# A graph attention layer on one core: exponentials in mid-step, joined rows loaded within the loop, quotients ahead in the last stage

## The chip, the core and the metric

The kernel runs on one core of one Trainium2 chip. The metric is the device time of one execution in microseconds, as the median of three runs. Five engines work beside each other, each on a queue of its own in program order: TensorE (PE, matrix products and transposes, with PEld for its weight loads), VectorE (DVE), ScalarE (ACT), GpSimd (POOL, here the issuer of indirect transfers) and SyncE (SP, the issuer of most other transfers). An instruction that waits holds up everything behind it on its engine.

## The reference

There are 12,500 nodes with 128 features and 400,000 edges, sorted by their target `dst`. For each edge:

```
h       = relu(layernorm(x))
message = (h @ w_src + b_src)[src] + (h @ w_dst)[dst]
message = message * edge_weight * radial_mlp(edge_attr_32)      # 32 -> 64 -> 64 -> 128, silu
message = message @ w_sep + b_sep                               # 8 heads x (16 alpha + 16 value)
score   = sum(smooth_leaky_relu(alpha) * alpha_dot)             # one per head
att     = segment_softmax(score, dst)                           # over the edges of one target
out     = segment_sum(value * att, dst) @ w_proj + b_proj
x       = x + out
```

The softmax's maximum and sum run over all edges with the same target, wherever they lie in the sorted list.

## The kernel before

**Tiling.** The edges are cut into 782 sections of 512; two sections are a pair, and the main loop takes one pair `k` per step, 391 (`NP`) steps. Features or channels lie on partitions, edges along the free dimension. Three constants order the loop: `MP = 8` pairs share one softmax group, `r = k % 8` is the step's place in its group, and `LAG = 13` is the number of steps by which the weighted values and their sums (`c = k - LAG`) run behind the messages of pair `k`.

**One step.** The order of the calls in `step(k)` is written by hand, and every engine follows it. `gather(k + 2)` (L867) has POOL bring 128 source rows per indirect transfer, eight per pair, into three buffers `gs0` and `gs1` for each half. `sources(k)` (L934) transposes the rows of this step on PE, which frees a buffer. `mlp1`, `mlp2` and `mlp3` (L886, L901, L918) are the radial net for pairs `k + 2`, `k + 1` and `k`, with `silu` on ACT (L890, L904; L904 comes once a step). `message` (L941, L948) adds the target rows and multiplies. `alphas` and `alphas_sum` (L954, L956, L961) make the activation of pair `k - 1`. In odd steps `scores` (L970, L987) makes the scores of two pairs; they go through a DRAM buffer `sc_d`, and at a group's end come back as `S` (L993) in another layout. `values` (L1065, L1067) multiplies the values of pair `c` with their weights, `one_hot` (L1051, L1054) marks the targets, and `sums` (L1078, L1082) adds them up into `ob` for a window of 64 nodes per section.

**The softmax group.** Once in eight steps, at the end of a step: `softmax_up` at `r = 2` (a product that spreads marks, L1003, and a running maximum on DVE, L1008), `softmax_down` at `r = 3` (L1013), then `softmax_exp` (subtraction on DVE, L1018, and the exponential on ACT, L1020). `softmax_T` at `r = 4` transposes the result (L1035) and copies it (L1038). ACT loads a table ahead of the exponential and another ahead of the next `silu`.

**Joining the windows.** Each section's sums are stored in section order into `agg`, the table of node rows (`store`, L1090), and whole windows into `win` (`store_win`, L1086). A target whose edges cross a section's end needs its parts joined. Thirteen blocks of 128 section ends do that (`block_load` to `block_out`, at fixed steps of the loop given by `LATE` and `stages`); eleven are finished in the loop and kept in `obs_d`. Behind the loop each is loaded into `comb` (L1364) and scattered by node number into `agg` (`scatter`, L1197), one per step of the 14 steps that bring the lagging values to an end; the last two blocks are made there. The tile framework orders accesses to `agg` by itself, unless a group declares that there is no dependence; in that queue a store waits for the scatter before it and the other way round.

**The last stage.** `final` loads `agg` in nine pieces of up to twelve blocks of 128 nodes (L1401), divides by the sum of weights (`quotients`: L1411, L1412, L1413 on DVE), and for 25 quads of four blocks transposes (L1424), copies (L1427), multiplies with `w_proj` (L1435), adds `x` (L1438) and stores (L1439). The quotients of the next twelve blocks are asked for in the middle of the three quads before.

Of the kernel before, what the change touches and what calls it, by code (L numbers as in the profile page):

```python
# [51 lines left out]
MQ = 2 * MP  # L52
LAG = 13


@with_exitstack
def gnn_kernel(ctx: ExitStack, tc: tile.TileContext, a: dict, out: bass.AP):
# [694 lines left out]
    def windows():  # L752
# [7 lines left out]
        with tc.tile_pool(name="ps", bufs=1, space=PSUM) as pp, \  # L760
# [254 lines left out]

            def softmax_exp(m):
                M = Ms[m]
                nc.vector.tensor_sub(M[:, 0, :], S_all[m], M[:, 1, :])  # L1018
                Ps[m] = sp.tile([P, SEC], F32, name="Pr", bufs=1)
                nc.scalar.activation(Ps[m], M[:, 0, :], AF.Exp)  # L1020
# [64 lines left out]
            def store_win(c):  # L1085
                nc.sync.dma_start(out=win[c * P:(c + 1) * P, :], in_=accs[c])  # L1086

            def store(c, f):
                at = nc.sync.value_load(base[0:1, f, c:c + 1])
                st = nc.sync.dma_start(out=agg[ds(at, W - 1), :], in_=accs[c][f * W:(f + 1) * W - 1, :])  # L1090
# [47 lines left out]
            def block_maxima(g):  # L1138
                w, node = width(g), nodes.pop(g)
                differ[g] = sp.tile([P, P + 1], BF16, name="differ", bufs=1)  # L1140
                nc.vector.tensor_tensor(differ[g][:, 0:w], node[:, 1:w + 1], node[:, 0:w], op=ALU.not_equal)
# [10 lines left out]
            def block_factors(g):  # L1152
# [4 lines left out]
                nc.vector.tensor_sub(mx, mx, up[:, 1:1 + w])  # L1157
                nc.scalar.activation(de, de, AF.Exp)
                nc.scalar.activation(mx, mx, AF.Exp)
                nc.vector.tensor_mul(mx[:, 1:w:2], mx[:, 1:w:2], differ.pop(g)[:, 1:w:2])  # L1160

            def block_columns(g):
# [6 lines left out]
                nc.tensor.transpose(pt[:, 1, 0:w], rx[:w, :], ident[:w, :w])  # L1169
                mx = mxs.pop(g)  # L1170
                tots[g] = [sp.tile([P, P], F32, name=n, bufs=2) for n in ("rn", "rd")]
                for k, r in enumerate(tots[g]):
# [22 lines left out]
            def scatter(g):  # L1195
# [5 lines left out]
                tc.declare_no_dep(st.ins, group="combined", reason="each node's row is written once")  # L1201
                tc.add_to_no_dep_group("combined", st.ins)

            comb = {}

            def combined(g):
# [3 lines left out]
            stages = {0: lambda g: (block_load(g), block_rows(g)), 2: block_maxima, 4: block_factors,  # L1210
                      5: block_columns, 6: block_totals, 8: block_out}
            assert LAST_M * MP == (NC - 1) * SB and NP - LAST_M * MP < MP and LATE + (NC - 3) * SB + 8 < NP

# [7 lines left out]
            def step(k):  # L1221
# [55 lines left out]
                if has(k + 2):  # L1277
                    mlp1(k + 2)
                if has(k):
                    mlp3(k)  # L1280
# [4 lines left out]
                if has(c - 1):  # L1285
                    sums(c - 1)
                    if k >= NP:
                        store_win(c - 1)
                        store(c - 1, 0)
                        store(c - 1, 1)  # L1290
# [37 lines left out]
                j, o = divmod(k - LATE, SB)  # L1328
                if 0 <= j < NC - 2 and o in stages:
                    stages[o](j)  # L1330

            for k in range(-5, NP):
                step(k)
            held.close()

# [6 lines left out]
            def out_rows(g):  # L1342
                block_rows_out(g, combined(g))
                scatter(g)

            jobs = {
                0: lambda: block_load(last - 1),
                1: lambda: block_maxima(last - 1),
                2: lambda: block_factors(last - 1),
                5: lambda: block_load(last),  # L1350
                6: lambda: block_maxima(last),
                7: lambda: (block_factors(last), block_rows(last - 1)),
                8: lambda: block_columns(last - 1),
                9: lambda: block_totals(last - 1),
                10: lambda: out_rows(last - 1),
            }
            assert SB * (NC - 1) + LAG + 1 == NP + 7
# [12 lines left out]
            block_rows(last)  # L1370
            block_columns(last)
# [7 lines left out]

    XQ = 12  # L1380
    out_v = out[0:NF * P, :].rearrange("(p t) c -> p t c", t=NF)
# [10 lines left out]
    def final(fp, x_fin, turned, product):  # L1392
        starts = list(range(0, NB, XQ))
        gs, qs, qTs = {}, {}, {}

        def load_g(i):

            gs[i] = fp.tile([P, XQ, ROW], F32, name="g", bufs=len(starts))
            for n, t0, t1 in blocks(starts[i], min(starts[i] + XQ, NB)):
                o = starts[i]  # L1400
                nc.sync.dma_start(out=gs[i][:n, t0 - o:t1 - o, :],  # L1401
                                  in_=agg_v[:, t0:t1, :] if n == P else agg[NF * P:N, :].unsqueeze(1))

        def quotients(i):
            r = fp.tile([P, XQ, H], F32, name="r")
            qs[i] = fp.tile([P, XQ, C], F32, name="q")
            g = gs.pop(i)
            for n, t0, t1 in blocks(starts[i], min(starts[i] + XQ, NB)):
                s = slice(t0 - starts[i], t1 - starts[i])
                m = t1 - t0  # L1410
                nc.vector.tensor_scalar(r[:n, s, :], g[:n, s, C:ROW], 1e-16, None, op0=ALU.add)  # L1411
                nc.vector.reciprocal(r[:n, s, :], r[:n, s, :])  # L1412
                nc.vector.tensor_mul(  # L1413
                    qs[i][:n, s, :].rearrange("p t (h k) -> p (t h) k", h=H),
                    g[:n, s, 0:C].rearrange("p t (h k) -> p t h k", h=H),
                    r[:n, s, :].unsqueeze(3).to_broadcast([n, m, H, C // H]))

        def turn(i):
            t0, t1 = quads[i]
            q, o = qs[t0 // XQ], t0 // XQ * XQ  # L1420
            pt = turned(i)
            for t in range(t0, t1):
                n = rows(t)
                nc.tensor.transpose(pt[:, t - t0, :n], q[:n, t - o, :], ident[:n, :n])  # L1424
            w = (t1 - t0 - 1) * P + rows(t1 - 1)
# [97 lines left out]
```

## Time and profile before

| | |
|---|---|
| three runs | 4210.71, 4211.2, 4215.71 us; median 4211.2 |
| the profiled execution's own time | 4210.06 us |
| its span, from the first to the last instruction | 4208.2 us |
| PE, DVE, POOL, ACT busy | 3917.1 (93%), 3103.4 (74%), 3009.4 (72%), 1901.6 (45%) us |
| mean granted clock of PE | 0.978 |
| first and last gather start | 73.65 and 4009.50 us |
| last stage, first quotient to last sum | 4142.28 to 4201.67 us |

The profile is of one execution. A row of a timeline gives the start in the span, the duration, engine, line, operation, what is written from what, and in brackets how long the engine was idle before and what ended that. A row of a group gives busy time and mean duration in ns, then the idle time before its instructions with what ended it. PE's busy time is that of pipelined products with modelled ends. Idle time on an engine that nobody waits for costs nothing.

### The profile page before, as it was taken

Reading aid. Unit: us, or ns where it says so; the run is one execution under the profiler, and the core shown is the slowest. Engines: PE = TensorE matmul, PEld = TensorE weight load, DVE = VectorE, ACT = ScalarE, POOL = GpSimd, SP = SyncE. Lnnn points to the kernel's source line nnn. Section 1 sums busy time; section 2 is a strip of 40 time slices with the busy share of each in tenths; the row PEclk is TensorE's granted clock in tenths of the full one; section 3 lists DMA queues with packets and bytes.
Section 4 is the critical chain, followed back from the end, with each engine's and each line's share of the span. In section 5 each row is a group of like instructions: output and inputs, shape, how many; then the busy total and the mean of one; then the engine's idle time right before and its main releaser. Section 6 shows DMA issues by size and latency. Waiting matters only on the chain. (4 is left out here: it accounts for less than half of the span.)

```text
span 4208.2 us, 87881 instructions
## 1 busy us (share of the span) xinstructions
PE 3917.1 (93%) x29351; PEld 2391.0 (57%) x29351; DVE 3103.4 (74%) x6187; ACT 1901.6 (45%) x4549; POOL 3009.4 (72%) x3195
## 2 busy tenths in 40 slices
PE   6789999999999999999999999999999999999975
PEld 6345555555555555555555555555555555555555
DVE  5567777777777777777777777777777777777754
ACT  5344444444444444444444444444444444444421
POOL 4767777777777777777777777777777777777710
PEclk8999999999999999999999999999999999999988
DMA  7766777777776776777777776776777676776624
GB/s 249 233 173 187 191 187 187 197 192 180 199 192 179 196 195 174 195 195 188 188 192 194 181 193 180 178 188 182 178 191 184 183 184 183 188 180 180 184 84 160
DMA packets 593334, 783.08 MB, mean 186 GB/s; under 512 B 125554, under 2 KB 392303, under 8 KB 592741
## 3 DMA queue, kind: packets, MB, share of 16 engines
q1 hardware_dynamic: 384786, 514.16, 40.9%
q0 software_dynamic: 100416, 205.44, 23.6%
q10 hardware_dynamic: 107666, 57.76, 4.6%
q8 instruction: 234, 3.83, 0.4%
q14 instruction: 232, 1.89, 0.2%
HBM read 637.83 MB, written 139.30 MB: 185 GB/s over the span
## 5 line engine op out<-in xcount | busy, mean ns | idle before, releaser
L867 POOL DMA_INDIRECT gs<-t_src,idx x3125 | 2971.5, 951 | 978.8 <-issue 801.7
L956 ACT ACTIVATE sl<-pa,c_b_a 128x512 f32<-128x512 f32 x782 | 536.9, 687 | 1021.1 <-PE pa L954 1009.5
L961 DVE SCALAR_TENSOR_TENSOR al<-pa,sl 128x512 f32<-128x512 f32 x782 | 539.8, 690 | 596.6 <-ACT sl L956 577.1
L1065 PEld LDWEIGHTS V<-c_w_v,mT 128*128 128x128 f32 x6048 | 746.7, 194 | 292.1 <-DVE ob L1082 119.1
L1065 PE MATMUL V<-c_w_v,mT 128*128 128x128 f32 x6048 | 879.3, 289 | 0.0
L954 PE MATMUL pa<-mT,c_w_a 128*128 128x512 f32 x1564 | 816.1, 604 | 4.0 <-DVE mT L948 3.0
L1067 DVE TENSOR_TENSOR pvx<-V,Pem 128x512 f32<-128x512 f32 x756 | 517.7, 685 | 243.8 <-PE V L1065 232.0
L934 PEld LDWEIGHTS pm<-ident,gs 128*128 128x128 f32 x3125 | 393.0, 142 | 422.1 <-issue 316.9
L1078 PEld LDWEIGHTS misc<-pvx,oh 128*64 128x64 f32 x6250 | 353.0, 137 | 407.8 <-ACT h L890 392.7
L926 DVE SCALAR_TENSOR_TENSOR rad<-p,c_fc_b,w_b 128x512 f32<-128x512 f32 x782 | 550.0, 745 | 40.1 <-PE p L918 3.5
L1078 PE MATMUL misc<-pvx,oh 128*64 128x136 f32 x6250 | 454.2, 287 | 115.4 <-ACT h L890 108.2
L948 DVE SCALAR_TENSOR_TENSOR mT<-pm,c_b_src,rad 128x512 f32<-128x512 f32 x782 | 550.6, 746 | 2.2 <-PE pm L941 2.2
L904 ACT ACTIVATE h<-p,b 128x512 f32<-128x512 f32 x391 | 287.6, 735 | 422.7 <-PE p L901 367.9
L934 PE MATMUL pm<-ident,gs 128*128 128x128 f32 x3125 | 471.0, 273 | 0.0
L918 PE MATMUL p<-h,w3b 64*128 64x512 f32 x1564 | 405.2, 595 | 14.4 <-ACT h L904 14.4
L941 PE MATMUL pm<-ohT,m 64*128 64x512 bf16 x2346 | 321.8, 380 | 0.0
L987 ACT ACTIVATE Sp<-m,b_s 128x512 f32<-128x512 f32 x192 | 131.9, 687 | 393.9 <-PE m L970 389.8
L886 PE MATMUL m<-eT,w1b 64*128 64x256 f32 x782 | 274.3, 431 | 17.9 <-DVE M L1008 16.7
L886 PE MATMUL misc<-eT,w1b 64*128 64x256 f32 x782 | 274.3, 431 | 0.0
L1051 DVE TENSOR_TENSOR oh<-lane,misc 128x504 f32<-128x504 f32 x391 | 261.3, 668 | 0.0
L901 PE MATMUL p<-h,w2b 64*64 64x256 f32 x3128 | 259.7, 402 | 1.0 <-DVE rad L926 1.0
L954 PEld LDWEIGHTS pa<-mT,c_w_a 128*128 128x128 f32 x1564 | 242.2, 196 | 20.0 <-DVE mT L948 7.1
(172 smaller groups left out, 3651.0 us busy)
## 6 DMA issues: line engine op xcount, KB each, us to landing
w_b<-in_edge_weight SPq DMA_DIRECT2D x390, 512.0 KB
d_b<-in_dst SPq DMA_DIRECT2D x390, 256.0 KB
gs<-t_src,idx POOLq DMA_INDIRECT x3125
e_t<-in_edge_attr ACTq DMA_DIRECT2D x390, 128.0 KB
sc_d<-Sp SPq DMA_DIRECT2D x192, 256.0 KB
win<-ob SPq DMA_DIRECT2D x391, 68.0 KB
agg<-ob SPq DMA_DIRECT2D x782, 33.5 KB
md<-t_dst SPq DMA_DIRECT2D x782, 32.0 KB
```

The lines of the kernel that those rows point to most:

```text
L867: nc.gpsimd.indirect_dma_start(out=gs[:, t, :], out_offset=None, in_=t_src[:, :], in_offset=bass.IndirectOffsetOnAxis(ap=idx[:, t0 + t:t0 ...
L886: nc.tensor.matmul(p1[q], w1b[s, :], eTs[k][s, :], start=True, stop=True)
L918: nc.tensor.matmul(p3s[k][:, f, 0:SEC], w3b[s, :], h2s[k][s, :], start=True, stop=True)
L926: nc.vector.scalar_tensor_tensor(rad[:, s], p3[:, f, 0:n], b3, w_g[k][:, s], op0=ALU.add, op1=ALU.mult)
L934: nc.tensor.matmul(pms[k, f][:, t * T:(t + 1) * T], gs[:, t, :], ident, start=(t == 0), stop=False, is_transpose=True, skip_group_check=True)
L948: nc.vector.scalar_tensor_tensor(mTs[k][:, s], pms.pop((k, f))[:, 0:n], b_n, rad[:, s], op0=ALU.add, op1=ALU.mult)
L954: nc.tensor.matmul(pa[:, 0:n], w_a, mTs[k][:, f * SEC:f * SEC + n], start=True, stop=True)
L956: nc.scalar.activation(sl[:, 0:n], pa[:, 0:n], AF.Silu, bias=b_a, scale=1.0)
L961: nc.vector.scalar_tensor_tensor(al, pa, 0.25, sl, op0=ALU.mult, op1=ALU.add)
L1065: nc.tensor.matmul(V[:, t, :], mTs[c][:, o:o + T], w_v, start=True, stop=True)
L1067: nc.vector.tensor_mul(pvx[c][:, f, 0:n, 0:C].rearrange("p t (h k) -> p t h k", h=H), V[:, 0:n, :].rearrange("p t (h k) -> p t h k", h=H), ...
L1078: nc.tensor.matmul(acc[f * W:(f + 1) * W, :], ohs[c][:, f * TS + t, :], pvx[c][:, f, t, :], start=(t == 0), stop=(t == n - 1), skip_group_ ...
```

## The change

Four things change together:

- `LAG` is 12. The softmax group is one step shorter: `softmax_up` moves to the middle of the step with `r = 2`, `softmax_down` and the subtraction (now `softmax_sub`) to its end, the exponential to the middle of the step with `r = 3` ahead of `mlp3`, and both `softmax_T` into that step. Table loads and exponentials of a block (`block_exp`) stand beside the large ones; the stages of a block are at other steps.
- The eleven finished blocks are loaded from `obs_d` in four transfers behind the steps `NP - 6` to `NP - 3`, into buffers of the edge loads (`bring`), and all are scattered behind the last gather. `order` declares by section which stores and scatters do not depend on each other.
- The rows of the last block are loaded two steps earlier as far as they exist; the last four come straight from `ob` (`last_rows_2`), not through `win`.
- In the last stage the pieces are of 1, 2 and then 3 quads, the quotients overwrite their inputs and are made up to four quads ahead of the sums, and transposes go two quads ahead.

```diff
-LAG = 13
+LAG = 12
+    EARLY_S = [(-(-2 * NS // P) - i) * (P // 2) for i in (2, 1)]
...
             def softmax_exp(m):
+                Ps[m] = sp.tile([P, SEC], F32, name="Pr", bufs=1)
+                nc.scalar.activation(Ps[m], Ms[m][:, 0, :], AF.Exp)
+
+            def softmax_sub(m):
                 M = Ms[m]
                 nc.vector.tensor_sub(M[:, 0, :], S_all[m], M[:, 1, :])
-                Ps[m] = sp.tile([P, SEC], F32, name="Pr", bufs=1)
-                nc.scalar.activation(Ps[m], M[:, 0, :], AF.Exp)
...
+            def order(ins, s, whole=False):
+                i = 1 if s < EARLY_S[0] else 2 if s < EARLY_S[1] else 3
+                for j in (1, 2):
+                    if j < i:
+                        tc.declare_no_dep(ins, group=f"early_{j}", reason="its rows follow those of the earlier sections")
+                    if i <= j:
+                        tc.declare_no_dep(ins, group=f"later_{j}", reason="its rows precede those of the later sections")
+                if whole and i < 3:
+                    tc.add_to_no_dep_group(f"early_{i}", ins)
+                if i > 1:
+                    tc.add_to_no_dep_group(f"later_{i - 1}", ins)
...
-                if 2 * c + 1 >= (NC - 1) * (P // 2):
-                    tc.declare_no_dep(st.ins, group="combined", reason="its rows follow those of the blocks")
+                order(st.ins, 2 * c)
...
+            def block_exp(g):
+                nc.scalar.activation(des[g], des[g], AF.Exp)
+                mx = mxs[g][:, 0:width(g)]
                 nc.scalar.activation(mx, mx, AF.Exp)
...
             stages = {0: lambda g: (block_load(g), block_rows(g)), 2: block_maxima, 4: block_factors,
-                      5: block_columns, 6: block_totals, 8: block_out}
+                      6: block_columns, 7: block_totals, 9: block_out}
...
+                if has(k - MP) and r == 3:
+                    softmax_exp(m - 1)
+                    if 0 <= j < NC - 2 and o == 5:
+                        block_exp(j)
                 if has(k):
                     mlp3(k)
...
+                if has(k - MP) and r == 2:
+                    softmax_up(m - 1)
                 if has(c):
                     values(c, 1)
-                if has(k - MP) and r == 4:
-                    softmax_T(m - 1, 0)
...
                     message(k)
+                if has(k - MP) and r == 3:
+                    softmax_T(m - 1, 0)
                 if has(k + 1):
                     mlp2(k + 1)
-                if has(k - MP) and r == 4:
-                    softmax_T(m - 1, 1)
                 if has(k - MP):
                     if r == 2:
-                        softmax_up(m - 1)
+                        softmax_down(m - 1)
+                        softmax_sub(m - 1)
                     elif r == 3:
-                        softmax_down(m - 1)
-                        softmax_exp(m - 1)
+                        softmax_T(m - 1, 1)
...
+            def bring(j):
+                g0, g1 = 3 * j, min(3 * j + 3, NC - 2)
+                t = lp.tile([P, 3, ROW], F32, name="e_t", bufs=4)
+                nc.sync.dma_start(out=t[:, 0:g1 - g0, :],
+                                  in_=obs_d[g0 * P:g1 * P, :].rearrange("(g p) c -> p g c", p=P))
+                for g in range(g0, g1):
+                    comb[g] = t[:, g - g0, :]
...
             for k in range(-5, NP):
                 step(k)
+                if 0 <= k - (NP - 6) < 4:
+                    bring(k - (NP - 6))
+                if k == NP - 3:
+                    for g in range(NC - 2):
+                        scatter(g)
...
+            def last_rows_2():
+                q = width(last) // 2
+                for i in range(2):
+                    nc.sync.dma_start(out=rrs[last][(i + 1) * q - 2:(i + 1) * q, :],
+                                      in_=accs[NP - 1][i * (W - 1):i * (W - 1) + W + 1:W, :])
...
-                if 0 <= j - 2 < NC - 2:
-                    nc.sync.dma_start(out=combined(j - 2), in_=obs_d[(j - 2) * P:(j - 1) * P, :])
-                    scatter(j - 2)
...
-        for i in range(len(starts)):
-            load_g(i)
-        quotients(0)
-        turn(0)
-        for i in range(Q):
-            if i % 3 == 1 and i // 3 + 1 < len(starts):
-                quotients(i // 3 + 1)
-            if i + 1 < Q:
-                turn(i + 1)
-            finish(i)
+        for j in range(len(parts)):
+            load_g(j)
+        made = 0
+        for i in range(-2, Q):
+            while made <= at[min(i + 4, Q - 1)]:
+                quotients(made)
+                made += 1
+            if i + 2 < Q:
+                turn(i + 2)
+            if i >= 0:
+                finish(i)
```

More of the change, by code (lines that the diff above doesn't have):

```diff
@@ L1139, in block_maxima @@
                 w, node = width(g), nodes.pop(g)
-                differ[g] = sp.tile([P, P + 1], BF16, name="differ", bufs=1)
+                differ[g] = sp.tile([P, P + 1], BF16, name="differ", bufs=2)
                 nc.vector.tensor_tensor(differ[g][:, 0:w], node[:, 1:w + 1], node[:, 0:w], op=ALU.not_equal)
@@ L1202, in scatter @@
                 tc.add_to_no_dep_group("combined", st.ins)
+                order(st.ins, g * (P // 2), True)
             comb = {}
@@ L1287, in step @@
                     if k >= NP:
-                        store_win(c - 1)
+                        if k == NP + LAG:
+                            last_rows_2()
+                        else:
+                            store_win(c - 1)
                         store(c - 1, 0)
@@ L1344, in out_rows, with last_rows @@
                 scatter(g)
+            def last_rows():
+                q, s = width(last) // 2, last * (P // 2)
+                rrs[last] = sp.tile([P, ROW], F32, name="rr", bufs=1)
+                for i in range(2):
+                    nc.sync.dma_start(out=rrs[last][i * q:(i + 1) * q - 2, :],
+                                      in_=rows_w[s:s + q - 2, i * (W - 1), :])
+            def last_rows_2():
+                q = width(last) // 2
+                for i in range(2):
+                    nc.sync.dma_start(out=rrs[last][(i + 1) * q - 2:(i + 1) * q, :],
+                                      in_=accs[NP - 1][i * (W - 1):i * (W - 1) + W + 1:W, :])
             jobs = {
@@ L1349, in windows @@
                 2: lambda: block_factors(last - 1),
[L1350 to L1355, printed above, removed]
+                3: lambda: block_exp(last - 1),
+                4: lambda: block_load(last),
+                5: lambda: block_maxima(last),
+                6: lambda: (block_factors(last), block_exp(last), block_rows(last - 1)),
+                7: lambda: block_columns(last - 1),
+                8: lambda: block_totals(last - 1),
+                9: lambda: out_rows(last - 1),
+                LAG - 1: last_rows,
             }
-            assert SB * (NC - 1) + LAG + 1 == NP + 7
+            assert SB * (NC - 1) + LAG + 1 == NP + 6
             for k in range(NP, NP + LAG + 1):
@@ L1369, in windows @@
                 pass
-            block_rows(last)
             block_columns(last)
@@ L1392, in final @@
     def final(fp, x_fin, turned, product):
[L1393 to L1411, printed above, removed]
+        ends_q = [1, 3] + list(range(6, Q, 3)) + [Q]
@@ new lines, in final, with load_g @@
+        parts = [(quads[a][0], quads[b - 1][1]) for a, b in zip([0] + ends_q, ends_q)]
+        at = [next(j for j, (t0, t1) in enumerate(parts) if t0 <= q0 < t1) for q0, _ in quads]
+        gs, qTs = {}, {}
+        def load_g(j):
+            t0, t1 = parts[j]
+            gs[j] = fp.tile([P, t1 - t0, ROW], F32, name=f"g{j}", bufs=1)
+            for n, u0, u1 in blocks(t0, t1):
+                nc.sync.dma_start(out=gs[j][:n, u0 - t0:u1 - t0, :],
+                                  in_=agg_v[:, u0:u1, :] if n == P else agg[NF * P:N, :].unsqueeze(1))
@@ L1412, in quotients @@
+        def quotients(j):
+            p0, p1 = parts[j]
+            r = fp.tile([P, 12, H], F32, name="r")
+            for n, t0, t1 in blocks(p0, p1):
+                s = slice(t0 - p0, t1 - p0)
+                nc.vector.tensor_scalar(r[:n, s, :], gs[j][:n, s, C:ROW], 1e-16, None, op0=ALU.add)
                 nc.vector.reciprocal(r[:n, s, :], r[:n, s, :])
[L1413 to L1416, printed above, removed]
+                q = gs[j][:n, s, 0:C].rearrange("p t (h k) -> p t h k", h=H)
+                nc.vector.tensor_mul(q, q, r[:n, s, :].unsqueeze(3).to_broadcast([n, t1 - t0, H, C // H]))
@@ L1418, in turn @@
         def turn(i):
             t0, t1 = quads[i]
-            q, o = qs[t0 // XQ], t0 // XQ * XQ
+            q, o = gs[at[i]], parts[at[i]][0]
             pt = turned(i)
@@ L1423, in turn @@
                 n = rows(t)
-                nc.tensor.transpose(pt[:, t - t0, :n], q[:n, t - o, :], ident[:n, :n])
+                nc.tensor.transpose(pt[:, t - t0, :n], q[:n, t - o, 0:C], ident[:n, :n])
             w = (t1 - t0 - 1) * P + rows(t1 - 1)
```

9 lines of the change are left out of this document (4 added, 5 removed).

## The prediction

> **What bounds the kernel now.** I read the page first, then the timeline of GpSimd (POOL) through the loop, then the steps of the loop on ScalarE (ACT) and TensorE (PE), then everything behind the last gather. The first row below is the page's group of gathers (busy, mean ns, idle before), the next four are POOL's timeline (start, us, what, idle before), the last is PE's.
>
> ```profile
> L867 POOL DMA_INDIRECT gs<-t_src,idx x3125 | 2971.5, 951 | 978.8 <-issue 801.7
> ...
> 73.65 1.18 POOL L867 DMA_INDIRECT gs<-t_src,idx  x1 [13.53 <-DMA t_dst<-ms]
> ...
> 4008.24 0.95 POOL L867 DMA_INDIRECT gs<-t_src,idx  x1 [0.30 <-issue]
> 4009.50 0.94 POOL L867 DMA_INDIRECT gs<-t_src,idx  x1 [0.30 <-PE V L1065]
> 4066.26 1.02 POOL L1197 DMA_INDIRECT agg<-comb,ids  x1 [55.82 <-PE pm L1065]
> 4035.72 0.27 PE L934 MATMUL pm<-ident,gs 128*128 128x128 f32 x1
> ```
>
> The gathers start 1.25 us apart (0.95 busy, 0.30 before it) and nothing but the next gather's own issue ends the time between them: eight steps of eight gathers cannot take less than 80.0 us. From the first to the last start 3124 intervals took 3935.9 us, 1.260 each. So most of the span runs at nearly the gathers' own pace; only 31 us (3935.9 - 3124 x 1.25) are lost to waits and slow gathers. The second thing to see is that PE transposes the last gathered tile at 4035.72, 26.2 us behind that gather's start: PE runs almost three steps late, as far as three buffers of `gs` allow. What follows has no gather in it.
>
> Why PE is late shows in the ACT timeline; L904 comes once a step.
>
> ```profile
> 2047.49 0.75 ACT L904 ACTIVATE h<-p,b 128x512 f32<-128x512 f32 x1 [1.00 <-PE p L901]
> ...
> 2057.39 0.74 ACT L904 ACTIVATE h<-p,b 128x512 f32<-128x512 f32 x1 [1.00 <-PE p L901]
> ...
> 2066.29 0.74 ACT L904 ACTIVATE h<-p,b 128x512 f32<-128x512 f32 x1 [1.00 <-PE p L901]
> ...
> 2072.56 0.69 ACT L987 ACTIVATE Sp<-m,b_s 128x512 f32<-128x512 f32 x1 [2.07 <-PE m L970]
> 2074.54 0.69 ACT L956 ACTIVATE sl<-pa,c_b_a 128x512 f32<-128x512 f32 x1 [1.29 <-PE pa L954]
> ...
> 2076.51 0.73 ACT L904 ACTIVATE h<-p,b 128x512 f32<-128x512 f32 x1 [1.00 <-PE p L901]
> 2077.26 1.28 ACT L1020 ACT_TABLE_LOAD   x1
> 2079.18 0.63 ACT L1020 ACTIVATE Pr<-M 128x512 f32<-128x512 f32 x1 [0.64 <-DVE M L1018]
> ...
> 2080.25 1.28 ACT L956 ACT_TABLE_LOAD   x1
> ...
> 2089.93 0.73 ACT L904 ACTIVATE h<-p,b 128x512 f32<-128x512 f32 x1 [1.00 <-PE p L901]
> ...
> 2127.78 0.74 ACT L904 ACTIVATE h<-p,b 128x512 f32<-128x512 f32 x1 [1.01 <-PE p L901]
> ```
>
> Steps take 9.90 (with scores), 8.90, 10.22, 13.42; eight take 80.29, against 80.0 of the gathers. PE and POOL are level, so PE never makes up its lag. The step of 13.42 is the one with the exponentials: 4.5 us over its kind.
>
> **Exponentials in mid-step.** Plain steps give 4 x (9.90 + 8.90) = 75.2 per eight. The change puts table load and exponential (1.28 + 0.63 = 1.91) where ACT idles 2.07 ahead of `Sp`, and the load back (1.28) where it idles 1.29 ahead of `sl`, in the same odd step. The subtraction moves a step ahead, so the 0.64 wait for it goes too. What stays on PE: two `spread` products (0.32 each, 10.22 - 9.90) and four transposes of `Pr`:
>
> ```profile
> L1035 PE MATMUL misc<-ident,Pr 128*128 128x128 f32 x196 | 46.7, 324 | 23.2 <-DVE oh L1054 20.2 <-ACT h L890 2.6 <-ACT Pem L1038 0.5
> L1008 DVE TENSOR_TENSOR_SCAN M<-m,S 128x512 f32<-128x512 f32 x49 | 59.4, 1212 | 16.8 <-DMA S<-sc_d 16.4 <-PE pm L1065 0.5
> L1018 DVE TENSOR_TENSOR M<-S,M 128x512 f32<-128x512 f32 x49 | 33.9, 692 | 1.7
> DVE al L961 <- ACT sl L956: 577.1, 728, 2.6
> ```
>
> 46.7 / 49 = 0.95. VectorE (DVE) now has upper scan (1.21) in mid-step and lower scan and subtraction (1.21 + 0.69) at the end of the same step. Behind them queue `pvx`, `al` and the messages, which PE needs; but DVE idles 0.79 ahead of each of two `al` a step, which swallows the first scan and most of the rest. One eight in four also has two small exponentials of a block there. I charge 1.0 for what is not swallowed (0 to 3.1, all of it). Sum: 75.2 + 0.64 + 0.95 + 1.0 = 77.8, 2.2 under the gathers' 80.0. Over 47 groups PE could make up 100 us; it needs some 21, from 26.2 down to about 5 (the gather's 0.94 and a landing; a small load below takes 1.9, the wait behind four tiles the rest). So the last tile is transposed **21 us** sooner (0 if PE stays above 80.0). POOL's own 31 lost us mostly stay: I take back **2** (-3 to 6), since the first softmax, whose scan waited 16.4, now blocks half a step earlier.
>
> A rule speaks against this place: the Trainium skill, "ScalarE: Activation LUTs", section "What ACT_TABLE_LOAD costs", gives each switch some 1.38 us of drain behind its 1.28. An estimate by that page: ACT would be 1.2 and 1.4 us late, and the eight steps 80.4. By that rule the time would be rival 1's. The trace disagrees so far: the load at 2077.26 starts 0.02 behind L904's end (2076.51 + 0.73). No run shows it in the new place.
>
> **Joined rows ahead, one lag step less.** Behind the loop the order is broken by scatters.
>
> ```profile
> 4066.82 1.15 PE L1078 MATMUL misc<-pvx,oh 128*64 128x136 f32 x16
> ...
> 4069.88 1.17 PE L1078 MATMUL misc<-pvx,oh 128*64 128x136 f32 x16
> ...
> 4093.72 2.08 PE L1065 MATMUL pm<-c_w_v,mT 128*128 128x128 f32 x8 [11.04 <-DVE pvx L1067]
> ...
> 4106.07 0.45 PE L1168 MATMUL misc<-ident,rr 128*128 128x128 f32 x1 [7.05 <-DMA rr<-win]
> ...
> 4125.45 1.80 SPq L1090 DMA_DIRECT2D agg<-ob  x2
> 4128.86 1.81 SPq L1090 DMA_DIRECT2D agg<-ob  x2
> 4124.61 0.30 DVE L1082 TENSOR_TENSOR ob<-misc,bare 128x136 f32<-128x136 f32 x1 [1.10 <-PE misc L1078]
> ```
>
> From 4035.72 to the last `ob` at 4124.61 are 88.9 us for 14 steps. An undisturbed step takes 3.06 (4066.82 to 4069.88), yet PE idles 18 in the two places shown, because SyncE (SP) holds stores, loads of `comb` and of the next blocks in one queue behind each scatter. In the changed program's order the eleven scatters stand directly behind the last gather (11 x 1.25 = 14 us on a POOL with nothing else to do), and SP's stores no longer wait for a scatter. Their four loads sit in SP's queue in the last loop steps, where nothing behind them is due before PE's next sums. With the smaller lag constant every value step runs one step sooner, at the same cost; one of 14 steps behind the loop is gone. Sum: from 4035.72 to the sixth step's sums (4066.82) were 31.1; with one step less, and 0.5 for the last softmax's scan in mid-step, 28.5. Eight more steps at 3.3, between PE's 3.06 and SP's 3.41 (4125.45 to 4128.86), are 26.4; the last two blocks' own work and waits 8 (4 to 16, PE's 7.05 twice over). 62.9: **26 us** (18 to 30).
>
> **Last rows and quotients.**
>
> ```profile
> 4130.84 0.75 SPq L1136 DMA_DIRECT2D rr<-win  x2
> 4132.77 0.30 ACT L1165 COPY rx<-rr 28x128 f32<-28x128 f32 x1 [13.82 <-DMA rr<-win]
> ...
> 4137.46 6.76 SPq L1401 DMA_DIRECT2D g<-agg  x10
> 4142.28 0.22 DVE r L1411
> ...
> 4157.84 0.13 DVE r L1411
> ...
> 4158.78 1.77 DVE q L1413
> ...
> 4163.57 0.69 DVE x_fin L1438
> ...
> 4201.20 0.47 DVE x_fin L1438 x2
> ```
>
> From `ob` to the first quotient are 17.7. The last rows now come straight from `ob`, not through `win`: `ob` 0.3, two direct row loads 0.7 to issue and 1.9 to land (two issues at 4130.84, use at 4132.77), 4.7 from there to the load of `g`, then 4 blocks instead of 12: 3 of the former 4.8 (1.9 to 4.8). 10.6: **7 us** (4 to 9).
>
> The last stage took 59.4 (4142.28 to 4201.67). The rows from 4142.28 on are the chain that ended last. Twelve blocks cost DVE 2.71 for quotients (4157.84 to 4160.55) and 2.07 for three sums, of a period of 6.42 (to 4164.26): the rest waits for PE, which waits for quotients. Ahead of time they hide each other: DVE 98 / 12 x 2.71 = 22.1, smaller parts 0.8, 25 sums 17.2, and half a period (3.2) for the first and last blocks' way through PE, an estimate: 43.3, **16 us** (12 to 18).
>
> Sum: 2 + 21 + 26 + 7 + 16 = 72 off the profiled execution's own 4210.06 is 4138; the median of the three runs lies 1.1 higher: **4139 us**.
>
> **Rivals.** (1) PE does not catch up: the mid-step group costs 2.2 more than I charge, as DVE's whole 3.1 would nearly do. POOL's pace holds, the 21 stay lost: 4160. For it: 80.29 and 80.0 lie close, and DVE carries more in one step. Against: the idle gaps fit. Chance 0.18.
>
> (2) The part behind the loop gives only part of it: the blocks' loads come late as before (16 instead of 8) and DVE and PE hide each other by half, (59.4 - 43.3) / 2 = 8 more: 4155. For it: SP's queue is as long as before but for the loads of `comb`. Chance 0.09.
>
> (3) Slower: the scan now stands behind the load of `S`.
>
> ```profile
> 219.15 0.58 SPq L993 DMA_DIRECT2D S<-sc_d  x1
> 222.70 1.22 DVE L1008 TENSOR_TENSOR_SCAN M<-m,S 128x512 f32<-128x512 f32 x1 [16.37 <-DMA S<-sc_d]
> 2056.25 0.56 SPq L993 DMA_DIRECT2D S<-sc_d  x1
> 2063.53 0.17 DVE L1054 TENSOR_TENSOR oh<-misc,far 128x8 f32<-128x8 f32 x1
> ```
>
> A load takes 3.55; the scan's new place is 7.4 behind its issue (2063.70). If SP issues it late so that every group waits d, PE's eight steps take 77.8 + d. Past d = 2.2 they outlast the gathers; 51 us of gain remain then, so from d = 3.3 on (48 groups) it is slower; d = 5 gives 4139 + 21 + 48 x 2.8 = 4294. For it: SP issues in order, so a store that waits holds the load up. Against: 3.9 of margin. Chance 0.05.
>
> (4) The scatters still hold SP up, as would show in waits of L1105: 4139 + 26 = 4165. Chance 0.02.
>
> My forecast has 0.66 and by itself 4122 to 4155. The range, 4118 to 4172, adds rivals 1 and 2 with weak ends. Some 0.2% (8.4 us) is what a measurement here tells from no change. Faster 0.94, same 0.01, slower 0.05.
>
> **What would show it.** Right: L905 steps in an eight of 80.0 with none of 13; last transposes about 5 behind the last gather; scatters at 1.25 right behind it; PE without idle over 3 behind them; `r` to the last sum in some 44. Wrong: PE's lag still 20 or more, `M` waiting for `S`, or agg stores waiting for scatters.

## The result and the profile after

| | before | after |
|---|---|---|
| median | 4211.74 us (4 runs, 4210.71 to 4215.71) | 4156.73 us (4 runs, 4153.83 to 4159.09) |
| ratio | | 0.9869, 95% interval 0.9856 to 0.9881 |
| profiled execution, its span | 4210.06, 4208.2 | 4158.83, 4157.1 |
| first to last gather start | 3935.85 | 3937.26 |
| last gather start to its transposition | 26.22 | 7.60 |
| to the start of the last `ob` | 88.89 | 67.79 |
| to the first quotient | 17.67 | 17.43 |
| to the end of the last sum | 59.40 | 46.96 |

The profiled execution gained 51.2 us of the 72 forecast, and each term came out smaller than its forecast. The five stretches of the table are used for every kernel below.

The last gather and the ends of the stretches behind it, from the timelines of POOL, PE and DVE of the changed kernel:

```profile
4010.52 0.95 POOL L868 DMA_INDIRECT gs<-t_src,idx  x1 [0.30 <-PE pm L935]
4018.12 0.27 PE L935 MATMUL pm<-ident,gs 128*128 128x128 f32 x1
4085.91 0.30 DVE L1085 TENSOR_TENSOR ob<-misc,bare 128x136 f32<-128x136 f32 x1 [1.80 <-DMA agg<-ob]
4103.34 0.18 DVE L1459 TENSOR_SCALAR r<-g 128x32 f32<-128x32 f32 x1 [8.23 <-DMA g<-agg]
```

PE transposes the last tile 7.6 us behind its gather, where it was 26.2.

ScalarE's timeline around one group of exponentials, with two rows of the `silu` that comes once a step, 32 steps apart, ahead of it:

```profile
283.63 0.75 ACT L905 ACTIVATE h<-p,b 128x512 f32<-128x512 f32 x1 [1.01 <-PE p L902]
...
595.74 0.74 ACT L905 ACTIVATE h<-p,b 128x512 f32<-128x512 f32 x1 [1.00 <-PE p L902]
...
2057.48 1.28 ACT L1019 ACT_TABLE_LOAD   x1
2058.78 0.63 ACT L1019 ACTIVATE Pr<-M 128x512 f32<-128x512 f32 x1
2059.35 0.69 ACT L988 ACTIVATE Sp<-m,b_s 128x512 f32<-128x512 f32 x1
2061.32 1.28 ACT L957 ACT_TABLE_LOAD   x1 [1.28 <-PE pa L955]
2062.61 0.69 ACT L957 ACTIVATE sl<-pa,c_b_a 128x512 f32<-128x512 f32 x1
```

While PE is late it takes (595.74 - 283.63) / 4 = 78.0 us for eight steps, under the gathers' 80.0. The first load and the exponential fill the gap ahead of `Sp`, as meant. The second load does not fill the gap ahead of `sl`: ACT idles 1.28, and the load comes behind the wait for PE, so it is not hidden.

The first group is another matter. Rows of SP, DVE and POOL:

```profile
219.27 0.58 SPq L994 DMA_DIRECT2D S<-sc_d  x1
222.80 1.22 DVE L1009 TENSOR_TENSOR_SCAN M<-m,S 128x512 f32<-128x512 f32 x1 [20.12 <-DMA S<-sc_d]
231.00 0.94 POOL L868 DMA_INDIRECT gs<-t_src,idx  x1 [15.20 <-PE pm L935]
```

The scores come no later than before (219.15 there), but the scan now stands half a step earlier and DVE waits 20.12 for them, where it waited 16.37. The hole in the gathers is 14.9 us over their pace (12.8 to 14.3 in five executions below whose kernels have the same first steps); it was 8.8.

Behind the loop, rows of POOL, ACT's queue, one stretch by itself (length, busy time of each engine, granted clock, DMA share, GB/s), SP, DVE and PE:

```profile
4011.77 1.02 POOL L1214 DMA_INDIRECT agg<-e_t,ids  x1 [0.30 <-issue]
...
4024.60 0.97 POOL L1214 DMA_INDIRECT agg<-e_t,ids  x1 [0.30 <-issue]
...
4043.09 0.36 ACTq L1436 DMA_DIRECT2D x_fin<-xb  x1
...
4044.47 0.33 ACTq L1436 DMA_DIRECT2D x_fin<-xb  x1
...
4045.00:4050.00 5.00, 4.92 (x51) 4.31 (x51) 3.67 (x9) 0.34 (x2) 0.00 (x0) 1.00 1.00 406
...
4044.76 0.37 SPq L1089 DMA_DIRECT2D win<-ob  x1
4050.39 4.10 SPq L1105 DMA_DIRECT2D agg<-ob  x2
...
4057.49 0.36 SPq L1139 DMA_DIRECT2D node<-ends_d  x1
...
4060.51 0.19 DVE L1155 TENSOR_TENSOR differ<-node 128x28 bf16<-128x28 int32 x1 [7.86 <-DMA node<-ends_d]
4061.91 2.08 PE L1068 MATMUL pm<-c_w_v,mT 128*128 128x128 f32 x8 [6.92 <-DVE pvx L1070]
```

The eleven scatters follow the last gather at 1.28 each, near the 1.25 forecast. Then three loads of `x_fin`, 896 KB each, leave ACT's queue within 1.4 us; ACT had waited with the last group's exponential (7.52, to 4037.31) and then for PE's transposes of it (3.52). For 5 us the DMA engines are full at 406 GB/s. Each store to `agg` waits for the one before to land, so SP stands still from 4045.1 to 4050.39, and the last block's load behind it is issued at 4057.49. DVE waits 7.86 for that, PE 6.92 for DVE.

From the last `ob` (4085.91) to the last scatter, rows of SP, ACT and POOL:

```profile
4091.48 1.19 SPq L1395 DMA_DIRECT2D rr<-ob  x2
4093.69 1.80 SPq L1105 DMA_DIRECT2D agg<-ob  x2
...
4095.62 0.26 ACT L1205 COPY comb<-misc 28x136 f32<-28x136 f32 x1 [1.57 <-PE misc L1204]
4097.78 0.90 POOL L1214 DMA_INDIRECT agg<-comb,ids  x1 [19.69 <-POOLq L1501]
```

The loads from `ob` are issued 5.6 us behind it, since SP is still at older stores. They also stand ahead of the last stores, and the last scatter starts 1.9 behind its data, 2.29 behind the end of those stores' issue (4095.49). Its rows overlap theirs.

### The profile page after: what moved, and what is told of

Read it like the earlier page. It is cut to its first block, busy times and chain, and to the rows that moved or that the text cites. A ratio compares the mean times of both kernels' runs of the same rounds, so it can differ in the third digit from the quotient of the medians.

```text
span 4157.1 us, 87940 instructions
## 1 busy us (share of the span) xinstructions
PE 3920.0 (94%) x29351; PEld 2371.7 (57%) x29351; DVE 3093.2 (74%) x6190; ACT 1895.5 (46%) x4549; POOL 3008.4 (72%) x3195
## 5 line engine op out<-in xcount | busy, mean ns | idle before, releaser
L1068 PEld LDWEIGHTS V<-c_w_v,mT 128*128 128x128 f32 x6064 | 738.2, 192 | 297.8 <-DVE ob L1085 154.2
L1068 PE MATMUL V<-c_w_v,mT 128*128 128x128 f32 x6064 | 868.3, 287 | 0.0
L955 PE MATMUL pa<-mT,c_w_a 128*128 128x512 f32 x1564 | 805.0, 597 | 3.9 <-DVE mT L949 2.8
L935 PE MATMUL pm<-ident,gs 128*128 128x128 f32 x3125 | 496.8, 276 | 71.6 <-DMA gs<-t_src,idx 69.7
L905 ACT ACTIVATE h<-p,b 128x512 f32<-128x512 f32 x391 | 288.2, 737 | 404.8 <-PE p L902 321.7
L1081 PE MATMUL misc<-pvx,oh 128*64 128x136 f32 x6250 | 452.5, 287 | 16.8 <-ACT h L891 12.5
L891 ACT ACTIVATE h<-misc,b 128x256 f32<-128x256 f32 x391 | 192.7, 493 | 143.5 <-PE misc L887 141.2
## 6 DMA issues: line engine op xcount, KB each, us to landing
agg<-ob SPq DMA_DIRECT2D x782, 33.5 KB
```

The source lines that it names most:

```text
L935: nc.tensor.matmul(pms[k, f][:, t * T:(t + 1) * T], gs[:, t, :], ident, start=(t == 0), stop=False, is_transpose=True, skip_group_check=True)
L955: nc.tensor.matmul(pa[:, 0:n], w_a, mTs[k][:, f * SEC:f * SEC + n], start=True, stop=True)
L1068: nc.tensor.matmul(V[:, t, :], mTs[c][:, o:o + T], w_v, start=True, stop=True)
L1081: nc.tensor.matmul(acc[f * W:(f + 1) * W, :], ohs[c][:, f * TS + t, :], pvx[c][:, f, t, :], start=(t == 0), stop=(t == n - 1), skip_group_ ...
```

## Experiments

`zero3`, `rows_win`, `x_split` and `all3` ran together on a chip on which the kernel before took 5308.55 us; the others on chips where it took 4210.0 to 4210.9. Only stretches behind the loop are read across that divide.

**Is it the place of the exponentials?** `exp_end`:

```diff
-                if has(k - MP) and r == 3:
-                    softmax_exp(m - 1)
...
                         softmax_sub(m - 1)
+                        softmax_exp(m - 1)
```

The call goes from mid-step to the end of the step with `r = 2`, and `block_exp` goes behind `block_factors` likewise.

> Exponentials of a group (and of a block) at the end of the step with the two scans, behind the subtraction, instead of half a step later; all else as in the changed kernel. Theory (the mid-step place is what lets TensorE catch up): eight steps of PE take 80 us or more again, one of them over 12 us; PE's lag behind the gathers stays 20 to 27 us to the end, instead of falling to 8 to 12; the last gathered tile is transposed some 15 to 18 us later; 4157 + 17 = 4174 us. Rival (the smaller lag constant and the earlier subtraction let it catch up, the place is indifferent): lag falls to about 10, 4157 within 4 us.

Measured: 4167.04 us (0.9893, 0.9876 to 0.9910). Rows of ACT, POOL and PE of this kernel:

```profile
2069.54 0.74 ACT L905 ACTIVATE h<-p,b 128x512 f32<-128x512 f32 x1 [1.00 <-PE p L902]
2070.30 1.28 ACT L1019 ACT_TABLE_LOAD   x1
2072.22 0.63 ACT L1019 ACTIVATE Pr<-M 128x512 f32<-128x512 f32 x1 [0.64 <-DVE M L1023]
...
2082.43 0.73 ACT L905 ACTIVATE h<-p,b 128x512 f32<-128x512 f32 x1 [0.25 <-PE p L902]
...
4011.26 0.95 POOL L868 DMA_INDIRECT gs<-t_src,idx  x1 [0.30 <-PE misc L887]
4032.25 0.27 PE L935 MATMUL pm<-ident,gs 128*128 128x128 f32 x1
```

The step over 12 us is back (12.89), and PE ends 21.0 behind the gathers. Of the 18.6 us by which the changed kernel is nearer, the place gives 13.4. The size is less sure than the sign: five executions whose kernels are the same up to there end 7.6 to 11.1 behind. The other 5.2 come with the shorter group or the lag constant; no run parts these two. They show in the steps as well: where the changed kernel's eight steps took 78.0, the same ones (`L905` at 283.16 to 599.70) take 79.1 here, not the 80 or more expected, and 79.8 in the kernel before. The time rose by 10, not 17: the lag is 13.4 longer, but in the profiled executions first to last gather is 1.3 and the last stage 1.6 shorter.

**Do the scatters hold SP up?** `scatter_tail` takes `bring` and the scatters out of the loop and loads and scatters one block a step behind it, as before; the declarations of `order` stay.

> Joined rows loaded and scattered one by one behind the loop, as in the kernel before; all else as changed. Theory (scatters between the stores hold SyncE up): PE idles 5 to 11 us in two or three places again, last transposition to last ob 80 to 86 us instead of 67.8; 4157 + 12 to 18 = 4172 us. Rival (SyncE's chain of stores to agg, each of which waits for the one before to land, sets the pace with or without scatters): 67.8 grows by no more than 3, 4160 us.

Measured: 4163.75 us (0.9891, 0.9875 to 0.9908); stretches 6.48, 72.05, 20.08, 45.30. So the place of the scatters is worth 4.3 and 2.7, 7 us in all, half of what the theory said. The waits of SP behind the loop tell why, first in the kernel before (from 4018 to 4140), then in this one (4015 to 4110); the columns are us in total, times, longest:

```profile
SPq L1090 <- DMA agg<-comb,ids: 21.3, 4, 11.9
SPq L1090 <- DMA agg<-ob: 13.0, 20, 3.6
```

```profile
SPq L1105 <- DMA agg<-ob: 21.0, 16, 4.4
```

Stores no longer wait for scatters even where scatters stand between them: the declarations alone took those 21.3 us away. What is left is the chain of stores that the rival names, though 72.05 is past its 3 us.

**Who holds the stores?** `x_behind` issues all eight loads of `x_fin` behind the last scatter.

```diff
-                if j >= 3:
-                    next(x_loads, None)
...
             out_rows(last)
+            for _ in x_loads:
+                pass
```

> The eight loads of x_fin (6.4 MB) issued behind the last scatter instead of one a step behind the loop; all else as changed. Theory (these loads fill the DMA engines, the stores to agg behind them land late, and the last block's load stands in SyncE's queue behind those stores): no store to agg waits over 2.5 us, PE's idle of 6.92 goes, last transposition to last ob 58 to 62 us instead of 67.8, last ob to the first load of g 2 to 3 shorter; the last stage pays the loads back, up to 16 us more. Rival (the stores are slow for themselves): 67.8 within 2 us, and the last stage longer.

Measured: 4159.15 us (0.9878, 0.9862 to 0.9895); stretches 11.04, 58.22, 21.18, 49.92. Without these loads the part behind the loop takes 58.2 instead of 67.8, 4.7 less than the prediction's 62.9. Rows of DVE, POOL and ACT's queue of this kernel:

```profile
4058.65 0.19 DVE L1155 TENSOR_TENSOR differ<-node 128x28 bf16<-128x28 int32 x1 [1.73 <-DMA node<-ends_d]
...
4080.77 0.30 DVE L1085 TENSOR_TENSOR ob<-misc,bare 128x136 f32<-128x136 f32 x1 [1.10 <-PE misc L1081]
4088.87 0.90 POOL L1214 DMA_INDIRECT agg<-comb,ids  x1 [14.01 <-POOLq L1499]
...
4086.71 2.12 ACTq L1434 DMA_DIRECT2D x_fin<-xb  x4
```

DVE's 7.86 for `node` is 1.73, and the last scatter starts 8.1 behind `ob` instead of 11.9. But the loads now stand ahead of that scatter's data and of `g`, and the 9.6 is given back there (3.8), in the last stage (3.0) and, in this execution, in the lag (3.4).

**The last stage.** `final_old` puts the old `final` back.

> The last stage as in the kernel before (quotients of twelve blocks into a tile of their own, made just before they are turned); all else as changed. Theory: first quotient to last sum 59 us instead of 47.0, 4157 + 12 = 4169 us. Rival (the prediction's size): the changed stage lost 3.7 us only to late loads, which the old order would meet too: 63 us from first quotient to last sum, 4173 us.

Measured: 4175.88 us (0.9921, 0.9904 to 0.9937); last stage 57.71 against 46.96, 10.8 us; the old stage has no late load to meet beyond its first. The time differs by 19.2; the profiled execution was the fastest of the four here (4173.46), and its other stretches sum to 3.4 more.

**The last rows.** `rows_win` loads them from `win`, behind the last store, as before.

> The last block's first and last rows loaded from win behind the loop, as in the kernel before, instead of partly from ob; all else as changed. Prediction's size: last ob to the first quotient 7 us longer than the changed kernel's 17.4. Theory now (SyncE is two steps behind ob at the end and the last scatter waits for the stores to agg anyhow, so the short way saves only the place in the queue): 2 to 3 us longer, 4159 to 4160 us. Rival (nothing): within 1 us.

Measured on the other chip: 5172.98 us (0.9747, 0.9730 to 0.9763); last `ob` to first quotient 17.55, where `zero3`, which has the change here, took 17.16. The short way from `ob` is worth 0.4 us as it stands, within the rival's 1 us.

**The first hole.** `zero3`:

```diff
-                if 0 <= 2 * k < NZ:
-                    for i in range(2 * k, min(2 * k + 2, NZ)):
+                if 0 <= 3 * k < NZ:
+                    for i in range(3 * k, min(3 * k + 3, NZ)):
```

> Rows of zeros for agg stored three a step instead of two, so that they are through three steps before the first softmax; all else as changed. Theory (the first group's scores wait in SyncE's queue behind the last zeros: the store of scores issued at 210.5 lands some 8 us later, and the scan in mid-step holds DVE 20 us for them): the scan waits under 6 us, the 14.9 us hole in the gathers shrinks to under 3, first to last gather 3937.3 becomes 3924 to 3928; 4157 - 11 = 4146 us. Rival (the scores are late for another load): the hole stays above 11, 4157 within 3 us.

Measured: 5179.61 us (0.9763, 0.9747 to 0.9779). On that chip PE sets the loop's pace, so the time says nothing about the hole. The profile says more: the scan's wait for `S` (5.6 in `rows_win`, with a hole of 5.0) is gone, but the gathers have a hole of 12.5 at 118.38, where the largest before the first scan was 4.5 in `rows_win`. The edit came again in `all4`, below.

**Fixes together, on the other chip.** `x_split` leaves four loads of `x_fin` behind the loop (at `j` 3, 6, 8 and 9) and puts four behind those of `g`; `all3` adds `zero3` and `nc.scalar` in place of `nc.sync` for the loads of the last rows.

> Four of the eight loads of x_fin stay behind the loop, in steps of their own (the 4th, 7th, 9th and 10th), the other four go behind the loads of g in SyncE's queue; all else as changed. Theory (three such loads at once fill the DMA engines and hold the stores to agg): last transposition to last ob 58 to 61 us instead of 67.8 (58.2 with none of them there), last ob to first quotient 14 to 17 instead of 17.4, the last stage 47 to 50; 4157 - 9 = 4148 us. Rival (what the tail gains the last stage loses, as with all eight behind the scatter): 4157 within 3 us.

Measured: 5172.93 us (0.9757, 0.9724 to 0.9791); stretches behind the loop 62.48, 14.42, 45.66, against 64.83, 17.16, 45.14 of `zero3`, which has these loads as in the changed kernel. The first gains 2.4, not the 7 to 10 expected, the second 2.7.

> Three a step of the zeros, the loads of x_fin split as in the run beside it, and the last block's rows loaded from ScalarE's queue, so that SyncE stores to agg without them ahead (the last scatter waited 1.9 us for those stores). If each does its part: -11, -9 and -2, 4135 us. If the hole at the first softmax is made up elsewhere in the loop, or the last stage takes the loads badly: 4146 to 4150 us.

Measured: 5151.96 us (0.9702, 0.9685 to 0.9718); 63.30, 12.36, 47.10. The last rows on ACT's queue let SP go straight to its stores: 2 us more off the way to the first quotient. That the last scatter waits for these stores shows across kernels: it starts 2.28 to 2.29 behind the end of their issue in the changed kernel, `x_behind`, `all4` and `x_late`, whatever its data do (1.1 behind them in the last, 1.9 in the first two).

**The changed kernel again, and the table load.** `after_again` is the changed kernel, `warm` adds one small activation behind `scores`, and `all4` is `all3` with it:

```diff
+                if has(k - MP) and r == 3 and k < NP:
+                    early = sp.tile([P, 1], F32, name="early", bufs=1)
+                    nc.scalar.activation(early, eps, AF.Silu)
```

> The changed kernel unchanged, beside the two variants that follow, on their chip, since the last four ran on a chip on which the kernel before took 5309 us. If this chip is like the first: 4157 within 3 us, hole at the first softmax 13 to 15 us, last transposition 7 to 9 us behind the last gather, 67 to 68 us from it to the last ob, 17 to the first quotient, 45 to 47 to the last sum. If it is like the second: some 5165 us, PE 40 us behind the last gather.

Measured: 4158.78 us (0.9876, 0.9859 to 0.9892); stretches 3940.56, 7.74, 66.10, 17.44, 45.50, hole 13.6.

> One more activation, of one element a partition, in the function of the sl, straight behind Sp in the step with the exponentials; all else as changed. In the changed kernel the load of the function's table stands behind the wait of sl for PE (idle 1.28 ahead of it, then 1.28 of load), so the load isn't hidden. Theory: the load now runs in that gap, sl comes 1.1 to 1.3 us sooner in one step of eight, PE's eight steps fall by about as much, so PE catches up faster (lag 16 us by step 40 instead of by step 52) and ends 1 us nearer the gathers; the time, on a chip where the gathers set the pace, 0 to 2 us less, 4155 to 4157. Where PE sets the pace: 48 x 1.2 = 58 us less. Rival (DVE's queue, not ACT, holds that step): nothing.

Measured: 4160.30 us (0.9877, 0.9859 to 0.9893); rows of ACT:

```profile
2065.68 1.28 ACT L1323 ACT_TABLE_LOAD   x1
2066.97 0.20 ACT L1323 ACTIVATE early<-eps 128x1 f32<-128x1 f32 x1
2067.08 0.67 ACT L957 ACTIVATE sl<-pa,c_b_a 128x512 f32<-128x512 f32 x1
```

The load now lies in the gap, and PE is within 12.0 of the gathers at step 52, where the changed kernel was 16.1 behind (19.1 in `after_again`). It ends 7.5 behind them all the same, and the time did not fall: the gathers set the pace.

> The early table load, three a step of the zeros, the loads of x_fin split (four behind the loop in steps of their own, four behind the loads of g), and the last block's rows loaded from ScalarE's queue. On a chip like the first: the hole at the first softmax goes from 14.9 us to under 3 (-11), last transposition to last ob from 67.8 to 58 to 61 (-8), last ob to first quotient from 17.4 to 12.4 as the run without the table load showed on the other chip (-5), last stage +1: 4157 - 23 = 4134 us. If the hole is only moved, 4145 us. On a chip like the second: about 5165 - 58 - 10 = 5097 us.

Measured: 4154.47 us (0.9865, 0.9849 to 0.9882), 4.3 under `after_again` on the same chip (4154.06 to 4155.28 against 4157.70 to 4160.72); stretches 3941.98, 8.85, 64.33, 12.73, 45.10. Rows of POOL and DVE:

```profile
168.16 0.94 POOL L868 DMA_INDIRECT gs<-t_src,idx  x1 [2.45 <-PE pm L935]
...
190.70 0.48 DVE L912 TENSOR_SCALAR ohT<-d_b,tgt 128x512 bf16<-128x512 int32 x1 [10.14 <-DMA d_b<-in_dst]
197.21 0.94 POOL L868 DMA_INDIRECT gs<-t_src,idx  x1 [7.29 <-PE pm L935]
232.60 0.94 POOL L868 DMA_INDIRECT gs<-t_src,idx  x1 [4.65 <-PE pm L935]
```

The hole of 13.6 became four of 2.2, 2.1, 7.0 and 4.4 over the pace, 15.6 in all; DVE waited 4.2 for `S`, and 10.1 for `d_b` ahead of it. More zeros a step move the wait to other loads, as in `zero3`: my theory that their removal closes the hole falls, and why transfers run late in the first steps stays open. Of the 23 us expected, 4 came.

**One more place for the loads of `x_fin`.** `x_late` has the last rows on ACT's queue, three loads at `j` 7, 8 and 9, and five behind those of `g`; zeros and table load as changed.

> Of the loads of x_fin three stay behind the loop, in its 8th, 9th and 10th step, past the loads that the last two blocks wait for; the other five go behind the loads of g. The last block's rows are loaded from ScalarE's queue. Zeros and table load as in the changed kernel. Theory (a load of x_fin costs what it stands ahead of: in the last run PE still idled 3.0 for node and 2.5 for rr, each behind one): both idles go, last transposition to last ob 58 to 61 us (66 to 68 in the changed kernel, 64.3 in the last run, 58.2 with no such load there), last ob to first quotient 12.5 to 13.5, last stage 45 to 48; on a chip like the first 4158 - 6 - 4 + 1 = 4149 us. Rival (three loads so late hold the last stores instead): last ob to first quotient over 15, 4153 to 4156 us.

Measured: 4150.89 us (0.9858, 0.9841 to 0.9874); stretches 3935.98, 11.13, 58.53, 15.10, 46.81. It is the fastest here. Behind the loop it is as quick as with no such load, but two of the three left ACT's queue together again, and SP's next stores waited for them. Rows of ACT's queue and SP:

```profile
4064.12 0.36 ACTq L1434 DMA_DIRECT2D x_fin<-xb  x1
4064.63 0.34 ACTq L1434 DMA_DIRECT2D x_fin<-xb  x1
...
4066.79 0.36 SPq L1089 DMA_DIRECT2D win<-ob  x1
4071.43 4.71 SPq L1105 DMA_DIRECT2D agg<-ob  x2
```

So the way to the first quotient took 15.1, between theory and rival.

## Why the prediction was right, and where it was off

The forecast was 4139 in a range of 4118 to 4172; 4156.7 came. That is inside the range, but 1.7 above the 4122 to 4155 that the forecast had by itself. Direction and the main mechanism held; every term was too large. Of the signs of being wrong only `M` waiting for `S` came, once in the loop. Of the signs of being right the scatters came as said; but PE idles over 3 behind them (6.92), the last transpose is 7.6 behind its gather, not about 5, and `r` to the last sum takes 47, not 44. Term by term, forecast and profile:

- **POOL's own loss, 2:** -1.0. I expected the first softmax to block half a step less. It blocked more: the scan moved ahead while its scores did not, DVE's wait grew by 3.75 and the hole by 6.1, while the other gathers lost 4.6 less than before. That is rival 3's mechanism, in one group; of the 49 scans only the first (20.1) and the last, behind the last gather (2.2), waited for scores:

```profile
L1009 DVE TENSOR_TENSOR_SCAN M<-m,S 128x512 f32<-128x512 f32 x49 | 59.6, 1217 | 22.3 <-DMA S<-sc_d 20.1 <-DMA S<-Sp 2.2
```

- **PE catches up, 21:** 18.6. Eight steps took 78.0 against my 77.8, and `exp_end` shows that the place does most of it. The floor was off. Taken at a step's fifth gather, which the last gather is too, PE is from there on 7 to 16 behind, on average between 9.2 (`r` = 0) and 11.1 (`r` = 5), and 7.6 at the end, not 5. A likely reason, not tested, is that its steps are uneven (8.2 to 12.8 us in the 32 timed above) and the gathers are not. The step "the load back (1.28) where it idles 1.29 ahead of `sl`" failed, without harm to the time (`warm`): the load took the wait with it. The Trainium skill's rule of "What ACT_TABLE_LOAD costs" ("ScalarE: Activation LUTs"), some 1.38 us of drain for each switch beside the load, isn't seen in the new place either: ACT idled 0.9 us in all ahead of 49 loads, and the exponential at 2058.78 starts 0.02 behind its load's end.

```profile
L1019 ACT ACT_TABLE_LOAD x49 | 62.9, 1283 | 0.9
L957 ACT ACT_TABLE_LOAD x48 | 61.6, 1283 | 55.7 <-PE pa L955 54.5 <-PE pm L935 1.2
```

- **Behind the loop, 26:** 21.1. The first part came as reckoned: the sums at 4046.61 stand 28.5 behind the last transposition, though PE idles 3.07 there for the last scan, where I had put 0.5, so the exact match is luck. The rest took 39.3, not 34.4. "The last two blocks' own work and waits 8" was the mis-sized term: 12.9, if the eight steps took their 26.4, halfway to rival 2's 16. I named SP's queue as the cause but not what fills it: the loads of `x_fin`, worth 9.6 (`x_behind`). Without them 58.2 would have beaten my 62.9.
- **Last rows, 7:** 0.2. I reckoned from `ob` as if SP were free. SP was still at older stores, and the last scatter had to wait for the stores that the new loads had been put ahead of.
- **Last stage, 16:** 12.4. The period of twelve blocks is 5.05 (from 4124.35 to 4129.40 below), where I took DVE's own 4.78; and the third part of `g` came 1.95 late. DVE is no longer what sets the period: it idles 0.46 in each for PE, and the chain that ended last runs through PE from 4106.64 to the last sums, with three products (0.89, 0.89, 0.91), three groups of transposes (0.63, 0.44, 0.44) and 0.85 in each period in which PE waits for nothing that the profile shows. What these 0.85 are stays open.

```profile
4108.54 0.21 DVE L1459 TENSOR_SCALAR r<-g 128x96 f32<-128x96 f32 x1 [1.95 <-DMA g<-agg]
...
4124.35 0.69 DVE L1484 TENSOR_TENSOR x_fin<-pa,x_fin 128x512 f32<-128x512 f32 x1 [0.46 <-PE pa L1481]
4129.40 0.69 DVE L1484 TENSOR_TENSOR x_fin<-pa,x_fin 128x512 f32<-128x512 f32 x1 [0.46 <-PE pa L1481]
```

Rival 2's 4155 lies nearest, but mostly by luck. It puts 8 more on the part behind the loop and 8 more on the last stage; 4.9 and 3.6 came. The rest of the 20.8 that were missing is 6.8 of the last rows, 3.0 of the gathers and 2.4 of the catch-up, none of which it prices. The late loads of the blocks that it names did come, for a reason that it does not name. Rival 1 did not come, rival 4's waits are gone.

## What to carry to other kernels

An engine that trails the one that sets the pace costs its lag once, at the end; small cuts to its cycle pay until the lag is gone and then nothing more (`warm`). When a wait is taken out of a queue, look at what else that queue's transfers share the DMA engines with: here large loads that nobody needed yet, let go in a bunch by a queue that had waited, held a chain of 33.5 KB stores. A term for a chain that starts at an engine's result has to start at the point where the issuing queue reaches it.

## What was not expected of the hardware

The same programs took some 1000 us longer on one chip, and the change gained more there (136 us: `rows_win`, which has the change but for the last rows, 5172.98 against 5308.55). The waits of PE of `rows_win` from 1000 to 4000 us show where; the columns are us in total, times, longest:

```profile
PE misc L1081 <- issue: 302.7, 166, 5.2
```

PE idles ahead of the sums for nothing that the profile shows, 1.8 us at a time; in the changed kernel on the first chip that row does not exist in the same stretch. This is 303 of PE's 539 us of idle there, against 98 in the changed kernel. A step also keeps PE busy for longer, 10.3 against 9.7 us, and the granted clock is lower, 0.97 against 1.00. PE, not the gathers, then sets the pace, and it stays 41 us behind to the end. Whether the clock is a cause or comes of the idle time, and what holds PE, stays open.

The table load came only when the activation behind it had its data: with the wait of `sl` for PE, ACT idled 1.28 and then loaded (54.5 us of such waits for PE ahead of 48 loads), and one activation of a column ahead of it was enough to put the load into that wait (`warm`).
